# Row transposes ahead of the outputs of the job in front, scatters regrouped, the last job's gates in two halves

## The chip, the cores and the metric

One core of a Trainium2 chip runs the kernel. The metric is the device time of one execution in microseconds (us); the time before is the median of three executions. The profile is of one further execution, and its own time stands beside it below.

## What is computed

Eight sequences of 512 tokens, 256 wide, go through four residual layers: attention to a 64-token context, a router that sends 384 of 512 tokens of each sequence through a gelu block, a second attention, and a mixture of eight experts of which each token uses two. The change touches the last layer alone:

```
x = hidden_states.reshape(-1, H)
probs = softmax(x @ gate_w.T)
w, idx = top_k(probs, 2)
w = w / sum(w)
combine = zeros((T, E)).at[arange(T)[:, None], idx].add(w)
def step(acc, inputs):
    gup, dn, ce = inputs
    g, u = split(x @ gup.T, 2)
    return acc + ce[:, None] * (silu(g) * u @ dn.T), None
```

All numbers are float32. The tokens are the 4096 rows of x, an expert's hidden width is 1024.

## The kernel before

**Rows and jobs.** When a batch (a sequence) has passed the second attention, its last steps, the route steps, write its rows into a table `xs` in HBM that is sorted by expert, and the plain rows into the output. Each row carries its token number, its expert and two weights beside the 256 values. `sent_off(t, k)` (L816) is one such scatter of 128 rows, issued by POOL as an indirect DMA; there are eight for each batch. The expert layer is then made of jobs: a job reads 256 rows of one expert (fewer in the small jobs), multiplies them with that expert's weights and adds the weighted result into the output by an indirect DMA from POOL (`add_rows`, L106).

**Early and late jobs.** Seven early jobs work on rows of the first four batches while the last four batches are still in the layers before. 18 late full jobs, seven jobs of 128 rows and ten pairs of 64 rows follow when every batch is through.

**The steps of an early job** (`early_steps`) are: `load` (SP reads two registers from the job list and issues the DMA of the rows into `e_xg`), four `load_piece` and one `load_down` (weights), then `enter` (TensorE transposes the rows into PSUM at L1111, ACT copies them to `e_xT` at L1114, VectorE makes token numbers and weights), four `gates` (two slices `gate_up` each, L1135, with L1143 on ACT and L1144 and L1145 on VectorE behind it), then `down(0)` and `down(1)` (the outputs: eight matmuls each at L1162, a scaling on VectorE at L1170, `add_rows` on POOL). There is one `e_xg`, one `e_xT`, one `e_hT` and one set of weights.

**The order.** All that happens up to the late jobs stands in an order written out by hand, the string `ORDER`. Each letter takes the next step of a chain: a digit is the attention, route and scatter chain of a batch, `j` the chain of the early jobs, `l` the making of the two job lists. `in_order` ties the instructions of each step behind those of the step before on TensorE, VectorE, ACT and POOL. A scatter also waits for the last TensorE instruction that stands before it in this order (`products[-1:]`). The SP queue issues its DMAs in the order of the program.

**The first late job.** `load(0, late=True)` issues the two halves of `wgu` (the gate and up weights, L1300), then the rows `xg` (L1277), then `wdn` (L1306); the rows wait until the eight scatters of the last batch have landed (`routed`). Then `enter(order[0], ...)` transposes them (L1317, ACT copy L1319) behind the last output of the last early job, and the gates of the late jobs (L1349, L1357, L1358) begin. Outputs of late jobs are `down` (L1406, L1414, L106).

**The late loop** takes each job in turn: its gates, the `enter` of the job after it, then the outputs of the job before it. So the last job's gates all stand before the outputs of the job in front of it, and its own outputs end the kernel. The first three jobs are pinned with `in_order`.

**Behind the last batch** POOL also writes zero rows into `xs` (L1032, L1034: the tails), which the rows of the pairs wait for (`tail_sent`).

Of the kernel before, what the change touches and what calls it, by code (L numbers as in the profile page):

```python
# [8 lines left out]
F32 = mybir.dt.float32  # L9
I32 = mybir.dt.int32  # L10
AF = mybir.ActivationFunctionType
ALU = mybir.AluOpType
# [3 lines left out]
P = 128  # L16
# [3 lines left out]
D = 256  # L20
H = 16
DK = 16
NC = D // P
# [4 lines left out]
E = 8  # L28
TOPK = 2
FF = 1024  # L30
NF = FF // P
# [4 lines left out]
RW = D + 4  # L36
# [18 lines left out]
64345645256352452222F36F35F63F222246455635547335546357453674356647435356733333556646v7l6  # L55
3333476G464jj77j5jGj666j5j7jj47Gjjj765j7457j4G5j64654j7j6556747j5j7644644444j76sH6jj5644
44j557j76j7j57jj7Hsj76jjjjHH7565j65jj676jj7jj6j57j5j6j75557j5555jj7j6j667j55557jjjs67j66
j76j7676j66j76s66667j7jjjj7jj6666j77j7j7jjjjj77jjs7j7j7j7j7j777jj77jjjljj77jj77jj
"""


# [1 line left out]
def xattn_ffn_kernel(ctx: ExitStack, tc: tile.TileContext, a: dict, out: bass.AP):  # L63
# [53 lines left out]
    with ExitStack() as front:  # L117
# [931 lines left out]
        def part_of_room(*shape):  # L1049
            n = 1  # L1050
            for k in shape:
                n *= k
            v = room[:, took[0] : took[0] + n]
            took[0] += n
            names = " ".join("abc"[: len(shape)])
            return v.rearrange(f"p ({names}) -> p {names}", **dict(zip("abc", shape)))
# [2 lines left out]
        e_xg = part_of_room(2, RW)  # L1059
        e_xT = part_of_room(NC, 2, P)  # L1060
        e_sg = [part_of_room(1, 2 * P)]
        e_now = keep.tile([P, 2, D], F32, name="e_now")
        e_w = {}
        piece = 2 * P

# [127 lines left out]
        chains["l"] = [early_list, full_list]  # L1193
        chains["j"] = early = []
        jobs_steps = [early_steps(j) for j in range(NEARLY)]
        early += jobs_steps[0][0]
        for j, (_, steps) in enumerate(jobs_steps):

            loads = list(jobs_steps[j + 1][0]) if j + 1 < NEARLY else []
            for n, step in enumerate(steps):  # L1200
                early.append(step)
                if loads and n != len(steps) - 2:
                    early.append(loads.pop(0))


        engines = (
# [5 lines left out]
        def in_order(step):  # L1212
            traced = nc.cur_bb.bb.instructions
            last = traced[-1].name
            step()
            made = []
            for i in reversed(nc.cur_bb.bb.instructions):
                if i.name == last:
                    break
                made.append(i)  # L1220
            for i in reversed(made):
                if i.engine not in engines:
                    continue
# [29 lines left out]
    def kind(j):  # L1253
        return "full" if j < NLATE else "one" if j < NLATE + NONE else "pair"

    def load(j, late=False):

        what = kind(j)
        subs, n = (2 if what == "full" else 1), (2 if what == "pair" else 1)
        first = j if what != "pair" else NLATE + NONE + 2 * (j - NLATE - NONE)  # L1260
        size = P if what != "pair" else P // 2

        with tc.issue_after(last.pop().ins) if last else nullcontext():
            at = [
                (
                    nc.sync.value_load(
                        jobs[0:1, 0, u : u + 1], min_val=0, max_val=E * QROWS + P - subs * size
                    ),
                    nc.sync.value_load(jobs[0:1, 1, u : u + 1], min_val=0, max_val=E - 1),
                )  # L1270
                for u in range(first, first + n)
            ]
        xg = moe.tile([P, 2, RW], F32, tag="xg", name=f"xg_{j}", bufs=3)

        def rows():
            for u, (row, _) in enumerate(at):
                i = nc.sync.dma_start(  # L1277
                    xg[u * size : u * size + size, 0:subs, :],
                    xs[bass.ds(row, subs * size), :].rearrange("(s p) w -> p s w", p=size),
                ).ins  # L1280

                if what == "pair":
                    after(i, tail_sent)
                else:
                    for other in tail_sent:
                        tc.declare_no_dep(i, other, reason="rows of tokens alone")
                    after(i, routed)

        if not late:
            rows()  # L1290
        w = []
        for u in range(n):
            pool = wpool[sets[0] % 4]
            sets[0] += 1
            wgu = pool.tile([P, NC, 2 * FF], F32, tag="wgu", name=f"wgu_{j}_{u}")
            wdn = pool.tile([P, NF, D], F32, tag="wdn", name=f"wdn_{j}_{u}")
            w.append((wgu, wdn))
        for (_, e), (wgu, _) in zip(at, w):
            for c in range(NC):
                nc.sync.dma_start(  # L1300
                    wgu[:, c, :], gu_t[bass.ds(e, 1), :, c, :].rearrange("e p o -> (e p) o")
                )
        if late:
            rows()
        for (_, e), (_, wdn) in zip(at, w):
            i = nc.sync.dma_start(wdn, dn_t[bass.ds(e, 1), :, :, :].rearrange("e p f o -> (e p) f o"))  # L1306
        last.append(i)
        return xg, w
# [31 lines left out]
    def gate_up_full(j, xT, w, hT=None, chunks=range(NF)):  # L1340
        wgu = w[0][0]
        if hT is None:
            hT = moe.tile([P, NF, 2 * P], F32, tag="hT", name=f"hT_{j}")
        for f in chunks:
            ps = ps_gu.tile([P, 2, 2 * P], F32, tag="gu", name=f"gu_{j}_{f}")
            for half in range(2):
                o = half * FF + f * P
                for c in range(NC):
                    nc.tensor.matmul(  # L1349
                        ps[:, half, :],  # L1350
                        lhsT=wgu[:, c, o : o + P],
                        rhs=xT[:, c].rearrange("p s q -> p (s q)"),
                        start=(c == 0),
                        stop=(c == NC - 1),
                    )
# [80 lines left out]
    assert sorted(order) == [j for j in range(NJOB) if j != spare]  # L1436

    def load_at(i):
        return load(order[i], i == 0) if i < len(order) else None

    loads = [load_at(0), load_at(1)]
    entered = []
    in_order(lambda: entered.append(enter(order[0], loads[0][0])))

    def placed(i, step):

        if i < NPIN:
            got = []
            in_order(lambda: got.append(step()))
            return got[0]  # L1450
        return step()

    pending = None
    for i, j in enumerate(order):
        w = loads.pop(0)[1]
        xT, tok, wt = entered.pop(0)
        if i > 0:
            loads.append(load_at(i + 2))
        if i == 0:

            hT = placed(i, lambda: gate_up_full(j, xT, w, None, range(NF // 2)))
            entered.append(placed(i, lambda: enter(order[1], loads[0][0])))
            placed(i, lambda: gate_up_full(j, xT, w, hT, range(NF // 2, NF)))
        elif j < NLATE:
            hT = placed(i, lambda: gate_up_full(j, xT, w))
        else:
            h, hT = placed(i, lambda: gate_up_rows(j, xT, w))
        if i == 0:
            small_list()
            unit_list()  # L1470
            loads.append(load_at(2))
        if 0 < i < len(order) - 1:
            entered.append(placed(i, lambda: enter(order[i + 1], loads[0][0])))
        if pending is not None:
            placed(i, lambda: down(*pending))
        if j >= NLATE:
            placed(i, lambda: turn(j, h, hT))
        pending = (j, hT, w, tok, wt)
# [55 lines left out]
```

## Time and profile before

| | us |
|---|---|
| median of three runs | 1164.99 (1164.78 to 1166.47) |
| the profiled execution's own time | 1173.17 |
| its span, first to last instruction | 1171.5 |
| TensorE (PE) busy | 1146.6 |
| VectorE (DVE) busy | 574.6 |
| ScalarE (ACT) busy | 372.9 |
| GpSimd (POOL) busy | 283.5 |
| gates of late full jobs, L1349, 1152 matmuls | 252.0 |
| outputs of late jobs, L1406, 1008 matmuls | 189.2 |
| gates of early jobs, L1135, 448 matmuls | 101.8 |
| adding rows into the output, L106, `now` | 98.5 (POOL) |
| scatters of rows into `xs`, L816 | 63.3 (POOL) |

All times of the profile count from the start of the span. A line of a timeline gives the start, the time taken, the engine, the line of the code, the operation, the tile written and those read, the shape, the number of instructions merged into the line (a float32 product appears as two matmuls), and in brackets the engine's idle time before it and what ended it. An engine name with a q is its instruction queue: SPq lines are issues of DMAs, not transfers. PEld is the loading of weights into TensorE. A window line gives, for a stretch of time, each engine's busy time and instructions in the order PE, PEld, DVE, ACT, POOL, then the clock that TensorE was granted (1.00 is full), and the share and rate of the DMA engines.

### The profile page before, as it was taken

How to read it: one execution, taken by the hardware profiler on the slowest of the kernel's cores; microseconds unless marked ns; L12 is line 12 of the kernel's file. 1: busy time of each engine (PE TensorE's matmuls, PEld its weight loads, DVE VectorE, ACT ScalarE, POOL GpSimd, SP SyncE). 2: the span in 40 equal slices, each digit the busy share in tenths (PEclk: the TensorE clock that was granted, in tenths of full speed). 3: DMA queues.
4: the chain of work that ended last, by engine and by line, in shares of the span. 5: the costliest groups of instructions: out<-in, count | busy, mean ns of one | idle time of the engine just before them, and what ended most of it. 6: DMA issues, size and time to landing. Idle time of an engine off the chain costs nothing. (4 is left out here: it accounts for less than half of the span.)

```text
span 1171.5 us, 20900 instructions
## 1 busy us (share of the span) xinstructions
PE 1146.6 (98%) x8010; PEld 825.0 (70%) x8010; DVE 574.6 (49%) x1664; ACT 372.9 (32%) x713; POOL 283.5 (24%) x307
## 2 busy tenths in 40 slices
PE   7999999999999999999999999999999999999997
PEld 3565666656657777778787876777767777677786
DVE  6898888878878676556722221221212222222211
ACT  3655645645543433232121121221111211112210
POOL 5331134123440411431412112112121121211212
PEclk9999999999999999999999999999999999999999
DMA  9000001010125344445789688896889967987711
GB/s 270 2 1 2 1 20 38 19 56 20 38 86 165 105 138 115 136 145 163 207 329 353 237 295 293 303 312 224 288 290 330 312 214 272 314 309 237 279 14 19
DMA packets 119988, 203.53 MB, mean 174 GB/s; under 512 B 10608, under 2 KB 105712, under 8 KB 108368
## 3 DMA queue, kind: packets, MB, share of 16 engines
q1 hardware_dynamic: 100048, 179.35, 43.5%
q0 software_dynamic: 14496, 17.86, 7.5%
q10 hardware_dynamic: 5344, 4.98, 1.3%
q8 instruction: 64, 1.05, 0.4%
q14 instruction: 36, 0.29, 0.1%
HBM read 180.38 MB, written 23.47 MB: 174 GB/s over the span
## 5 line engine op out<-in xcount | busy, mean ns | idle before, releaser
L1349 PE MATMUL gu<-xjT,wgu 128*128 128x256 f32 x1152 | 252.0, 379 | 0.7 <-ACT xjT L1319 0.7
L1349 PEld LDWEIGHTS gu<-xjT,wgu 128*128 128x128 f32 x1152 | 217.6, 190 | 31.0 <-issue 1.2
L106 POOL DMA_INDIRECT out_dram<-now,tok x63 | 98.5, 1564 | 474.6 <-DVE now L1414 296.4
L1406 PE MATMUL o<-wdn,hT 128*128 128x256 f32 (+1 forms) x1008 | 189.2, 380 | 0.0
L1406 PEld LDWEIGHTS o<-wdn,hT 128*128 128x128 f32 (+1 forms) x1008 | 151.1, 173 | 28.3 <-issue 1.7
L1358 DVE TENSOR_TENSOR hT<-sg,gu 128x256 f32<-128x256 f32 x144 | 60.6, 421 | 190.6 <-ACT sg L1357 186.7
L1357 ACT ACTIVATE sg<-gu 128x256 f32<-128x256 f32 x144 | 55.3, 384 | 208.5 <-PE gu L1349 205.7
L1376 PE MATMUL gr<-wgu,xjT 128*64 128x512 f32 (+1 forms) x432 | 120.8, 596 | 0.0
L1135 PE MATMUL gu_e<-x_sb,e_wgu 128*128 128x256 f32 x448 | 101.8, 382 | 0.8 <-ACT x_sb L1114 0.6
L1135 PEld LDWEIGHTS gu_e<-x_sb,e_wgu 128*128 128x128 f32 x448 | 83.8, 190 | 15.9 <-issue 2.8
L1414 DVE TENSOR_SCALAR now<-o,wt 128x256 f32<-128x256 f32 x53 | 25.6, 483 | 137.1 <-PE o L1406 137.1
L1376 PEld LDWEIGHTS gr<-wgu,xjT 128*64 128x64 f32 (+1 forms) x432 | 42.8, 150 | 68.4 <-issue 67.0
L390 POOL TENSOR_TENSOR rstd<-ve,mhalf 128x4 f32<-128x4 f32 x32 | 33.0, 1031 | 233.0 <-DVE ve L388 185.4
L816 POOL DMA_INDIRECT xs<-xr,slots x64 | 63.3, 989 | 105.0 <-issue 35.3
L483 DVE TENSOR_REDUCE mx<-sc 128x32 f32<-128x2048 f32 x32 | 73.2, 2287 | 21.4 <-PE sc L476 17.9
L1386 DVE TENSOR_TENSOR h<-sg,gr 128x512 f32<-128x512 f32 x34 | 23.4, 687 | 83.5 <-PE gr L1376 83.4
L446 PE MATMUL ps_q<-xT,w_wq 128*128 128x512 f32 x128 | 62.0, 612 | 0.5 <-ACT xT L417 0.5
L577 PE MATMUL py<-w_wo,cT 128*128 128x256 f32 x256 | 60.3, 384 | 0.0
L1385 ACT ACTIVATE sg<-gr 128x512 f32<-128x512 f32 x34 | 20.3, 597 | 124.7 <-PE gr L1376 124.7
L577 PEld LDWEIGHTS py<-w_wo,cT 128*128 128x128 f32 x256 | 47.3, 190 | 11.7 <-issue 5.3
L399 ACT ACTIVATE xn<-x_sb,shift,rstd 128x256 f32<-128x256 f32 x96 | 49.8, 594 | 17.9 <-DVE shift L396 16.6
L385 DVE BATCH_NORM_STATS2 st<-x_sb 128x6 f32<-128x256 f32 x128 | 51.3, 401 | 4.9 <-DMA x_sb<-in_x_dram 4.8
(286 smaller groups left out, 1455.8 us busy)
## 6 DMA issues: line engine op xcount, KB each, us to landing
wgu<-in_guT_dram SPq DMA_DIRECT2D x90, 1024.0 KB
wdn<-in_dnT_dram SPq DMA_DIRECT2D x45, 1024.0 KB
e_wgu<-in_guT_dram SPq DMA_DIRECT2D x56, 256.0 KB
e_wdn<-in_dnT_dram SPq DMA_DIRECT2D x7, 1024.0 KB
xg<-xs SPq DMA_DIRECT2D x18, 260.0 KB
out_dram<-x_sb ACTq DMA_DIRECT2D x8, 512.0 KB
x_sb<-in_x_dram SPq DMA_DIRECT2D x7, 512.0 KB
x_sb<-xs SPq DMA_DIRECT2D x7, 260.0 KB
```

Source lines behind the costliest of these rows:

```text
L106: i = nc.gpsimd.indirect_dma_start(out=out_rows, out_offset=bass.IndirectOffsetOnAxis(ap=tok, axis=0), in_=rows, in_offset=None, bounds_ch ...
L385: nc.vector.bn_stats(st, x_sb[:, b * TB + t, :])
L446: nc.tensor.matmul(ps, lhsT=w["wq"][:, k, c * P : (c + 1) * P], rhs=got["xT"][:, k, :], start=(k == 0), stop=(k == NC - 1),)
L483: nc.vector.tensor_reduce(got["mx"].rearrange("p t (r h) -> p r t h", r=NQ)[:, :, :, 2 * c : 2 * c + 2], sc, AX.X, ALU.max,)
L577: nc.tensor.matmul(py[:, s, :], lhsT=cT[:, c, t * P : (t + 1) * P], rhs=w["wo"][:, c, :], start=(c == 0), stop=(c == NC - 1),)
L816: i = nc.gpsimd.indirect_dma_start(out=xs, out_offset=bass.IndirectOffsetOnAxis(ap=slots[:, t, k : k + 1], axis=0), in_=xr[:, t, :], in_of ...
L1135: nc.tensor.matmul(ps[:, half, :], lhsT=e_w["gu"][:, c, o : o + P], rhs=e_xT[:, c].rearrange("p s q -> p (s q)"), start=(c == 0), stop=(c ...
L1349: nc.tensor.matmul(ps[:, half, :], lhsT=wgu[:, c, o : o + P], rhs=xT[:, c].rearrange("p s q -> p (s q)"), start=(c == 0), stop=(c == NC - 1),)
L1357: nc.scalar.activation(sg[:, 0 : 2 * P], ps[:, 0, :], AF.Silu)
L1358: nc.vector.tensor_tensor(hT[:, f, :], sg[:, 0 : 2 * P], ps[:, 1, :], ALU.mult)
L1376: nc.tensor.matmul(ps[rows], lhsT=xT[:, c, 0, rows], rhs=wgu[:, c, o : o + 4 * P], start=(c == 0), stop=(c == NC - 1),)
L1406: nc.tensor.matmul(ps[rows], lhsT=hT[:, f, s * P + rows.start : s * P + rows.stop], rhs=wdn[:, f, :], start=(f == 0), stop=(f == NF - 1),)
```

## The change

1. In every early job `enter` is put one step sooner: behind the gates and ahead of the two outputs of the job in front of it. The loads keep their places.
2. The first late job gets its own tiles (`first_xT`, `first_tok`, `first_wt`). Its rows go into `e_xg`: `first_rows` reads the job list and issues them on SP right before the first gates of the last early job, ahead of that late job's `wgu`. `first_enter` transposes them ahead of the last early job's outputs, instead of behind them, with a `ps_m` buffer.
3. The end of `ORDER` is changed. Before, the last eight scatters stood in pairs among the steps of the last two early jobs. Of these eight, now six stand ahead of the outputs of the last but one early job and two behind them; the steps of the last early job have none among them.
4. In the late loop the last job's gates are cut in two halves, with the outputs of the job in front between them.

In the built program this is what moves. On TensorE nothing is added or removed: the four transposes of each `enter` change places with the sixteen matmuls of `down(0)` and `down(1)`, and at the end two outputs stand between gate slices four and five. On SP the rows of the first late job now stand ahead of both `wgu` halves, not behind them. On POOL the order at the end of the early part was scatter 2, output, scatter 2, output, scatter 4, output 2, tails; it is scatter 6, output 2, scatter 2, output, tails, output.

```diff
-j76j7676j66j76s66667j7jjjj7jj6666j77j7j7jjjjj77jjs7j7j7j7j7j777jj77jjjljj77jj77jj
+j76j7676j66j76s66667j7jjjj7jj6666j77j7j7jjjjj77jjs7j7j7j7j7j777j77j77jj77jljjjjjj
...
+        def first_rows():
+            with tc.issue_after(last.pop().ins):
+                first_at.append((
+                    nc.sync.value_load(jobs[0:1, 0, 0:1], ...),
+                    nc.sync.value_load(jobs[0:1, 1, 0:1], ...),
+                ))
+            i = nc.sync.dma_start(
+                e_xg, xs[bass.ds(first_at[0][0], 2 * P), :].rearrange("(s p) w -> p s w", p=P)
+            ).ins
+            last.append(i)
...
+            after(i, routed)
+        def first_enter():
+            ps = ps_m.tile([P, NC, 2, P], F32, tag="m", name="ps_e_first")
+            for c in range(NC):
+                for k in range(2):
+                    nc.tensor.transpose(ps[:, c, k, :], e_xg[:, k, c * P : (c + 1) * P], ident)
+            nc.scalar.copy(first_xT, ps)
+            nc.vector.tensor_copy(first_tok, e_xg[:, :, D].bitcast(I32))
...
-        early += jobs_steps[0][0]
+        early += jobs_steps[0][0] + jobs_steps[0][1][:1]
         for j, (_, steps) in enumerate(jobs_steps):
             loads = list(jobs_steps[j + 1][0]) if j + 1 < NEARLY else []
-            for n, step in enumerate(steps):
+            for n, step in enumerate(steps[1:-2]):
+                if loads:
+                    early.append(loads.pop(0))
+                elif n == 0:
+                    step = lambda step=step: (first_rows(), step())
                 early.append(step)
-                if loads and n != len(steps) - 2:
-                    early.append(loads.pop(0))
+            if loads:
+                early.append(loads.pop(0))
+                early.append(jobs_steps[j + 1][1][0])
+                early += steps[-2:] + loads
+            else:
+                early += [lambda step=steps[-2]: (first_enter(), step()), steps[-1]]
...
-        xg = moe.tile([P, 2, RW], F32, tag="xg", name=f"xg_{j}", bufs=3)
+        xg = moe.tile([P, 2, RW], F32, tag="xg", name=f"xg_{j}", bufs=3) if j > 0 else None
...
-    in_order(lambda: entered.append(enter(order[0], loads[0][0])))
+    entered = [(first_xT, first_tok, first_wt)]
...
+        elif i == len(order) - 1 and j < NLATE:
+            hT = gate_up_full(j, xT, w, None, range(NF // 2))
+            down(*pending)
+            pending = None
+            gate_up_full(j, xT, w, hT, range(NF // 2, NF))
```

More of the change, by code (lines that the diff above doesn't have):

```diff
@@ L1061, in xattn_ffn_kernel @@
         e_sg = [part_of_room(1, 2 * P)]
+        first_xT = part_of_room(NC, 2, P)
         e_now = keep.tile([P, 2, D], F32, name="e_now")
+        first_tok = keep.tile([P, 2], I32, name="first_tok")
+        first_wt = keep.tile([P, 2], F32, name="first_wt")
+        first_at = []
+        def first_rows():
+            with tc.issue_after(last.pop().ins):
+                first_at.append((
+                    nc.sync.value_load(
+                        jobs[0:1, 0, 0:1], min_val=0, max_val=E * QROWS + P - 2 * P
+                    ),
+                    nc.sync.value_load(jobs[0:1, 1, 0:1], min_val=0, max_val=E - 1),
+                ))
[3 more added lines that the diff above has]
+            last.append(i)
+            for other in tail_sent:
+                apart(i, [other], "rows of tokens alone")
+            after(i, routed)
[6 more added lines that the diff above has]
+            nc.vector.tensor_copy(first_tok, e_xg[:, :, D].bitcast(I32))
+            wt2 = small.tile([P, 2], F32, tag="wt2", name="wt2_first")
+            ej = job_e[:, 0:1]
+            nc.vector.scalar_tensor_tensor(
+                first_wt, e_xg[:, :, D + 1], ej, e_xg[:, :, D + 2], ALU.is_equal, ALU.mult
+            )
+            nc.vector.scalar_tensor_tensor(
+                wt2, e_xg[:, :, D + 1], ej, e_xg[:, :, D + 3], ALU.not_equal, ALU.mult
+            )
+            nc.vector.tensor_tensor(first_wt, first_wt, wt2, ALU.add)
         e_w = {}
@@ L1254, in kind, with load @@
         return "full" if j < NLATE else "one" if j < NLATE + NONE else "pair"
-    def load(j, late=False):
+    def load(j):
         what = kind(j)
@@ L1261, in load @@
         size = P if what != "pair" else P // 2
-        with tc.issue_after(last.pop().ins) if last else nullcontext():
-            at = [
+        with tc.issue_after(last.pop().ins) if last and j > 0 else nullcontext():
+            at = first_at if j == 0 else [
                 (
@@ L1272, in load @@
             ]
-        xg = moe.tile([P, 2, RW], F32, tag="xg", name=f"xg_{j}", bufs=3)
[L1275 to L1290, printed above, removed]
+        xg = moe.tile([P, 2, RW], F32, tag="xg", name=f"xg_{j}", bufs=3) if j > 0 else None
+        for u, (row, _) in enumerate(at) if j > 0 else []:
+            i = nc.sync.dma_start(
+                xg[u * size : u * size + size, 0:subs, :],
+                xs[bass.ds(row, subs * size), :].rearrange("(s p) w -> p s w", p=size),
+            ).ins
+            if what == "pair":
+                after(i, tail_sent)
+            else:
+                for other in tail_sent:
+                    tc.declare_no_dep(i, other, reason="rows of tokens alone")
+                after(i, routed)
         w = []
@@ L1302, in load @@
                 )
-        if late:
-            rows()
         for (_, e), (_, wdn) in zip(at, w):
@@ L1438, in load_at @@
     def load_at(i):
-        return load(order[i], i == 0) if i < len(order) else None
+        return load(order[i]) if i < len(order) else None
     loads = [load_at(0), load_at(1)]
-    entered = []
-    in_order(lambda: entered.append(enter(order[0], loads[0][0])))
+    entered = [(first_xT, first_tok, first_wt)]
     def placed(i, step):
```

## The prediction

> **What bounds the kernel now.** I read the busy table first, then the timeline of TensorE where the early part ends, then POOL's and SP's at the same place, then the last ten microseconds.
>
> ```profile
> PE 1146.6 (98%) x8010; PEld 825.0 (70%) x8010; DVE 574.6 (49%) x1664; ACT 372.9 (32%) x713; POOL 283.5 (24%) x307
> ```
>
> TensorE is the bound: 1146.6 of 1171.5 us. The change adds and removes no matmul, so it can only gain or lose in the 24.9 us that are left. 5.2 of these lie before the first matmul and 7.3 behind the last. The rest are holes. From 400 us on, the timeline of TensorE shows three of more than a third of a microsecond, and they sit where the change works:
>
> ```profile
> 551.17 7.07 PE L1162 MATMUL o_e<-e_wdn,x_sb 128*128 128x256 f32 x32
> 558.07 0.60 PE L1111 MATMUL ps_e<-ident,x_sb 128*128 128x128 f32 x4
> ...
> 559.40 14.21 PE L1135 MATMUL gu_e<-x_sb,e_wgu 128*128 128x256 f32 x64 [0.61 <-ACT x_sb L1114]
> 573.46 7.43 PE L1162 MATMUL o_e<-e_wdn,x_sb 128*128 128x256 f32 x32
> 581.67 0.63 PE L1317 MATMUL ps_x<-ident,xg 128*128 128x128 f32 x4 [0.79 <-DMA xg<-xs]
> 582.97 7.17 PE L1349 MATMUL gu<-xjT,wgu 128*128 128x256 f32 x32 [0.68 <-ACT xjT L1319]
> ```
>
> The gates of the last early job wait 0.61 us for the copy of its transposes. The first late job waits 0.79 for its rows and 0.68 for its copy. Behind 582.97 TensorE is never idle until the end (50.00 of each 50 us), so whatever moves that start moves the end by the same amount.
>
> **What the whole change could gain.** Had the first late job nothing to wait for, its gates would start at 558.80 (where the last early job's gates can begin: outputs, transposes and one small counting product are the same work in either order and end there today, 0.61 ahead of 559.40) + 14.06 (those gates, 559.40 to 573.46) + 0.44 (four transposes, start to start as 558.07 to 558.51) + 6.90 (two outputs, 551.17 to 558.07) = 580.20 against 582.97: 2.8 us. That is all there is.
>
> **Part 1, the early jobs' transposes one step sooner.** In jobs two to six other products stand between the transposes and the gates, and the only such hole in the trace is the 0.61 us. It goes: gates start at 558.80 and TensorE reaches 572.85, not 573.46. Rows of those jobs are loaded a whole job ahead (job seven's: issued at 535.90, used at 558.07, now at 551.2), so no wait replaces it. VectorE's five small instructions (558.68 to 559.67, 1.0 us) move ahead of the two scalings; these wait 1.0 us longer, hidden by POOL, which takes them later anyway (below). If that cover were gone it would cost POOL 1.0 us.
>
> **Parts 2 and 3, rows of the first late job and the scatters.** This is the expensive part.
>
> ```profile
> 557.33 1.05 POOL L816 DMA_INDIRECT xs<-xr,slots  x1 [20.92 <-issue]
> 558.68 1.01 POOL L816 DMA_INDIRECT xs<-xr,slots  x1 [0.30 <-PE ps_e L1111]
> 560.00 1.62 POOL L106 DMA_INDIRECT out_dram<-e_now,tok_e  x1 [0.31 <-DVE cnt_f L915]
> ...
> 575.66 0.96 POOL L816 DMA_INDIRECT xs<-xr,slots  x1 [0.30 <-issue]
> ```
>
> ```profile
> 567.01 0.91 SPq L1300 DMA_DIRECT2D wgu<-in_guT_dram  x2
> 578.62 0.39 SPq L1277 DMA_DIRECT2D xg<-xs  x1
> ```
>
> The rows may be read once the eighth scatter has landed. It starts at 575.66, ends at 576.62, and SP issues the rows at 578.62: 2.00 us. Their transposes start at 581.67: another 3.05. Today the scatters are held back by products of the last early job; afterwards they follow one another. The first cannot be sooner: VectorE finishes the slots and columns at 556.45, unchanged. So: scatter one 557.33, two 1.35 later, three to six every 1.28 (561.93 to 563.22 is 1.29, 410.60 behind 409.33 is 1.27): six starts at 563.80 and ends at 564.76. Then two outputs of 1.62 with 0.30 before each: 568.60. Scatter seven 568.90, eight 570.17, ending 571.13; it starts 5.5 sooner than now. SP issues the rows at 573.13, and the transposes can start at 576.18.
>
> But TensorE now comes to these transposes at 572.85, ahead of 6.90 us of outputs that would have covered the wait. It stands 3.33 us, with the outputs queued behind the transposes. Then 576.18 + 0.44 + 6.90 = 583.52: the copy is hidden, and the gates still begin 0.55 later than now. The 0.37 us by which the outputs of the last early job take longer today (7.43 against 7.07) go too; 580.20 above has that in it. Bounds: the first scatter starts 0.88 behind VectorE, an output at 1133.92 only 0.28 behind (1133.64), so at best 0.6 sooner; a landing that holds up POOL at the end takes from 1159.66 to 1163.27, 3.61 instead of 2.00, so at worst 1.6 later. I take the sum's own row, the same scatter with no weights in flight.
>
> **The clock.** A long hole on TensorE has a price of its own:
>
> ```profile
> 16.92 1.17 PE L476 MATMUL sc<-kbd,qT 32*128 32x128 f32 x32
> ...
> 21.30 0.33 PE L414 MATMUL ps_x<-ident,xn 128*128 128x128 f32 x1 [1.29 <-ACT xn L399]
> ...
> 24.03 2.03 PE L476 MATMUL sc<-kbd,qT 32*128 32x128 f32 x32
> ```
>
> ```profile
> 19.04:22.45 3.41, 1.79 (x6) 0.55 (x4) 3.22 (x10) 1.81 (x4) 1.83 (x3) 1.00 1.03 337
> 22.45:25.86 3.41, 3.27 (x38) 2.73 (x37) 2.28 (x3) 1.44 (x3) 3.23 (x7) 0.50 1.08 345
> 237.50:240.91 3.41, 1.95 (x16) 1.05 (x19) 3.38 (x5) 0.00 (x0) 0.61 (x1) 1.00 0.18 65
> ```
>
> In a stretch of 3.41 us TensorE was busy for 1.79; in the next, its granted clock (the column behind the five engines) is 0.50, and 32 small matmuls take 2.03 instead of 1.17. With 1.95 busy it kept its clock. Both stretches lie on one grid of 3.41 us, which also has 571.99, 575.41 and 578.82. A hole from 572.85 to 576.18 leaves 0.86 busy in the first: half clock from 575.41 to 578.82, of which 2.64 us are work, so 1.32 us are lost. Wherever the grid lies, one stretch holds at least 1.67 of the 3.33 us, so the loss is 0.83 to 1.71 (half of 1.67 to 3.41). I take 1.32.
>
> [...]
>
> **The weights** of the first late job stand behind its rows now: issued from 573.7 (0.59 behind the rows, as 578.62 to 579.21 on SP) instead of 567.01. Before, both halves were in by the stretch from 575.41, where the DMA share falls from 0.82 to 0.22: 8.4 to at most 9 us, so 582.1 to 582.7, and the gates need them at 583.5 or, with the clock, 584.8. Nothing, with 0.8 to 2.7 us of cover; each microsecond beyond is one lost. POOL's last output now stands behind the tails; the first to need it landed is the scatter at 616.27.
>
> **Part 4, the end.**
>
> ```profile
> 1160.79 0.48 DVE L1414 TENSOR_SCALAR now<-o,wt 128x256 f32<-128x256 f32 x1 [2.97 <-PE o L1406]
> 1163.27 1.56 POOL L106 DMA_INDIRECT out_dram<-now,tok  x1 [3.61 <-issue]
> 1164.24 0.48 DVE L1414 TENSOR_SCALAR now<-o,wt 128x256 f32<-128x256 f32 x1 [2.97 <-PE o L1406]
> 1165.13 1.56 POOL L106 DMA_INDIRECT out_dram<-now,tok  x1 [0.30 <-DVEq L1483]
> ```
>
> The next to last scatter waits for the job in front to land and so holds POOL until 1164.83; the last starts at 1165.13, 0.41 behind its scaling (1164.72) where 0.28 would do. With the job in front 7 us sooner, 0.13 is gained. The last four slices' tails (0.39 on ACT, 0.42 on VectorE, 0.87 us behind the product at 1150.4) are needed only by the eighth of eight products, 3.0 us in: nothing; 0.9 if uncovered.
>
> **Sum**: +0.55 + 1.32 - 0.13 = +1.74 us on a span of 1171.5, thus 1173.2 (execution 1174.9). The profiled execution is 8.2 us longer than the median; a difference within 25 us of it I carry over as it is: 1164.99 + 1.74 = **1166.7**.
>
> **Rivals.**
> - *The clock falls for two stretches.* The stretch from 575.41 is itself idle for 0.77 us; no row shows whether 77% busy at half clock brings the clock back (96% did, at 25.86). Decides if it doesn't: 3.41/2 = 1.71 more, 1168.4, slower. For it: 57% busy kept the full clock, which speaks against; nothing else.
> - *The weights come late.* Decides past 585.4, 11.7 us behind their issue instead of 8.4 to 9: against it, the two scatters that shared the engines then are gone; for it, the rows' 260 KB go first. 1167.4 and up, slower.
> - *Short hole, no drop.* Outside the profiler POOL may issue faster, as 8.2 us go somewhere. Below about 1.5 us of hole the clock stays: 0.55 - 1.8 - 0.13 = -1.4; with 3.33 and the clock kept +0.42. Between them, 1163.6 to 1165.4, within 0.2% of before.
> - *No hole at all*, the scatters 3.33 us (24% of 13.8) sooner: 1162.1, faster. Against: a chain of fixed spacings.
>
> **How the numbers follow.** One clock stretch 0.42 (1166.2 to 1167.1), two stretches 0.22, weights 0.08, short hole or kept clock 0.18, no hole 0.10. 0.2% (2.3 us) is about what a measurement of this kernel can tell from no change. Within it lie 0.42 + 0.18 = 0.60; slower 0.30; faster 0.10. The range leaves out the fastest case and the worst of the weights: 1164.0 to 1168.8.
>
> **What would show it.** Right: a hole of 3 us at `ps_e_first` released by the DMA of the rows, the last scatter near 570, a stretch of 0.50 clock behind it, gates of the first late job at 584 to 585, no holes behind it. Wrong: that hole under 1.5 us, clock 1.00 throughout, gates before 582, or a hole at the first `gu` released by `wgu`.

## The result: 0.4% slower, and the profile after

| | before | after |
|---|---|---|
| median of the runs of one chip, us | 1165.86 (1164.78 to 1167.04, 6 runs) | 1170.81 (1169.83 to 1171.76, 6 runs) |
| ratio of after to before, 95% interval | | 1.0042 [1.0031, 1.0052] |
| the profiled execution's own time, us | 1173.17 | 1170.64 |
| its span, us | 1171.5 | 1168.9 |
| first gates of the first early job (first `gu_e`), us | 352.61 | 344.34 |
| from there to the first late output (first `o`), us | 258.75 | 264.48 |
| from the first late output to the end of the last matmul, us | 552.85 | 552.84 |

The change costs 4.95 us (3.6 to 6.1). The two profiled executions say the opposite at first sight, since the span after is the shorter. But before its first early gates, where both kernels run the same instructions, the execution of before was 8.3 us behind. The stretch that the change touches, from the first early gates to the first late output, took 258.75 us before and 264.48 after. I call it *the way* below, and compare kernels by it; what lies behind it is equal to 0.01 us up to the last matmul.

The first line of the page's busy table, of the kernel after:

```profile
PE 1145.0 (98%) x8010; PEld 823.8 (70%) x8010; DVE 574.5 (49%) x1664; ACT 372.7 (32%) x713; POOL 282.9 (24%) x307
```

Same matmuls, same engine as the bound. What is new are holes. The timeline of TensorE after has them at the outputs and transposes of jobs in the middle of the early part, which the prediction had down as free of waits:

```profile
375.62 1.14 PE L414 MATMUL ps_x<-ident,xn 128*128 128x128 f32 x8 [0.50 <-ACT x_sb L1152]
...
453.88 2.43 PE L1200 MATMUL o_e<-e_wdn,x_sb 128*128 128x256 f32 x10 [0.86 <-DVE e_now L1208]
...
483.34 1.07 PE L476 MATMUL sc<-kbd,qT 32*128 32x128 f32 x32
484.34 0.64 PE L715 MATMUL ps_g<-xT,gwT 128*32 128x128 f32 x16
484.91 0.65 PE L1149 MATMUL ps_e<-ident,x_sb 128*128 128x128 f32 x4
486.82 0.66 PE L491 MATMUL pm<-ident,mx 128*128 128x128 f32 x4 [1.25 <-DVE mx L483]
```

The same place of the third hole in the timeline of before, and the reduction that `pm` waits for, in VectorE's timeline after:

```profile
490.47 1.07 PE L476 MATMUL sc<-kbd,qT 32*128 32x128 f32 x32
491.46 0.64 PE L715 MATMUL ps_g<-xT,gwT 128*32 128x128 f32 x16
492.04 3.72 PE L1162 MATMUL o_e<-e_wdn,x_sb 128*128 128x256 f32 x16
495.60 0.60 PE L491 MATMUL pm<-ident,mx 128*128 128x128 f32 x4
```

```profile
484.47 2.29 DVE L483 TENSOR_REDUCE mx<-sc 128x32 f32<-128x2048 f32 x1 [0.29 <-PE sc L476]
```

Between the scores `sc` and the transposes `pm` of their maxima, VectorE needs 2.29 us. Before, the first output of an early job, 3.6 us long, stood there and covered them. After, the four transposes `ps_e` stand there, 0.5 us long. That is what putting `enter` one step sooner does in this kernel: the letters of `ORDER` keep their places, so `enter` takes the letter of `down(0)`, `down(0)` that of `down(1)`, and `down(1)` that of the load behind it, other batches' steps between. The last load (`load_down`) takes the letter that `enter` had, so not every load keeps its place. The outputs come later, and the reduction that they used to cover is bare.

The other two holes have the same origin, but what is waited for there is a buffer in PSUM, where this kernel has its products written. ACT's and VectorE's lines that end them, in the kernel after:

```profile
375.00 0.56 ACT L1152 COPY x_sb<-ps_e 128x512 f32<-128x512 f32 x1
```

```profile
453.35 0.48 DVE L1208 TENSOR_SCALAR e_now<-o_e,wt_e 128x256 f32<-128x256 f32 x1
```

The products named in these two cases take their buffers in turn from one pool of four, `ps_m`, so by the program each takes the buffer of the fourth product before it. Both start right behind the instruction that reads that product, 0.06 and 0.05 us behind its end. `ps_x` at 375.62 reads nothing of the early rows, but three buffers (`ctx`, `pz`, `ctx`) were taken between `ps_e` and it, and the copy of `ps_e` ends at 375.56. The second output at 453.88 has three buffers (`ps_x`, `pc`, `ps_x`) between the first output and itself, and the scaling of the first ends at 453.83. Before, the two outputs of that job had only `bz` between them. This is read from the program and the trace; no run changed the number of buffers.

The end of the early part after: TensorE, then POOL's last scatter, SP's issue of the rows, and the last scaling on VectorE.

```profile
561.14 7.17 PE L1173 MATMUL gu_e<-x_sb,e_wgu 128*128 128x256 f32 x32 [0.29 <-DVE x_sb L1183]
570.50 1.09 PE L1089 MATMUL ps_e_first<-ident,x_sb 128*128 128x128 f32 x4 [2.19 <-DMA x_sb<-xs]
571.38 8.30 PE L1200 MATMUL o_e<-e_wdn,x_sb 128*128 128x256 f32 x32
580.46 7.14 PE L1389 MATMUL gu<-x_sb,wgu 128*128 128x256 f32 x32 [0.78 <-DVE e_now L1208]
```

```profile
564.79 1.00 POOL L816 DMA_INDIRECT xs<-xr,slots  x1 [0.30 <-issue]
```

```profile
567.68 0.38 SPq L1077 DMA_DIRECT2D x_sb<-xs  x1
568.33 0.91 SPq L1342 DMA_DIRECT2D wgu<-in_guT_dram  x2
```

```profile
579.72 0.48 DVE L1208 TENSOR_SCALAR e_now<-o_e,wt_e 128x256 f32<-128x256 f32 x1 [0.88 <-PE o_e L1200]
```

The foreseen hole is there, 2.19 us instead of 3.33. The rows were issued 1.89 us behind the last scatter's end (565.79) and used 2.82 later. Behind the hole the outputs take 8.30 us, not 7.07. Then comes a hole that the prediction did not have: the first late gates wait 0.78 us for the scaling of the last output, which makes neither their rows nor their weights. The windows of that place:

```profile
567.04:570.45 3.41, 1.27 (x6) 0.77 (x5) 3.29 (x14) 0.87 (x3) 0.00 (x0) 1.00 0.50 131
570.45:573.86 3.41, 3.36 (x10) 2.93 (x11) 2.21 (x12) 0.59 (x1) 0.00 (x0) 0.50 0.99 413
573.86:577.27 3.41, 3.41 (x17) 2.98 (x16) 1.00 (x5) 0.00 (x0) 0.24 (x1) 1.00 1.00 365
```

One stretch with the clock at 0.50 (the column behind the five engines), as foreseen, and only one.

### The profile page after: what moved, and what is told of

Same layout as the page of the kernel before. It is cut to its first block, busy times and chain, and to the rows that moved or that the text cites. A ratio compares the mean times of both kernels' runs of the same rounds, so it can differ in the third digit from the quotient of the medians.

```text
span 1168.9 us, 20905 instructions
## 1 busy us (share of the span) xinstructions
PE 1145.0 (98%) x8010; PEld 823.8 (70%) x8010; DVE 574.5 (49%) x1664; ACT 372.7 (32%) x713; POOL 282.9 (24%) x307
## 5 line engine op out<-in xcount | busy, mean ns | idle before, releaser
L1389 PE MATMUL gu<-xjT,wgu 128*128 128x256 f32 x1088 | 238.1, 379 | 0.0
L1389 PEld LDWEIGHTS gu<-xjT,wgu 128*128 128x128 f32 x1088 | 205.6, 190 | 28.5 <-issue 1.2
L106 POOL DMA_INDIRECT out_dram<-now,tok x61 | 95.0, 1558 | 450.7 <-DVE now L1454 306.6
```

The source lines that it names most:

```text
L106: i = nc.gpsimd.indirect_dma_start(out=out_rows, out_offset=bass.IndirectOffsetOnAxis(ap=tok, axis=0), in_=rows, in_offset=None, bounds_ch ...
L1389: nc.tensor.matmul(ps[:, half, :], lhsT=wgu[:, c, o : o + P], rhs=xT[:, c].rearrange("p s q -> p (s q)"), start=(c == 0), stop=(c == NC - 1),)
```

## The experiments

Theory 1, as it was put down before the first of these runs: part 1 costs 1.5 to 2.5 us, since outputs stand one letter later and no longer cover what they covered; parts 2 and 3 cost 2.5 to 3.3 us, for the rows, the clock and a PSUM buffer; part 4 costs nothing. The runs were made in three groups, each on a chip of its own and with the kernel before beside it (medians of 1172.0, 1174.0 and 1172.3 us); each ratio is to the before of its own group. The table collects them; "way" and "idle" (TensorE's idle time within the way) are of each kernel's own profiled execution.

| kernel | way, us | idle, us | ratio to before, 95% |
|---|---|---|---|
| before, the trace shown | 258.75 | 3.57 | |
| before again | 257.93 | 3.04 | 0.9998 [0.9987, 1.0009] |
| part 4 alone | 258.32 | 3.15 | 1.0006 [0.9994, 1.0017] |
| part 1 alone | 262.06 | 5.67 | 1.0042 [1.0030, 1.0053] |
| part 1 alone, again | 261.81 | 5.59 | 1.0038 [1.0023, 1.0053] |
| parts 2 and 3 alone | 259.67 | 4.94 | 1.0028 [1.0017, 1.0038] |
| parts 2 and 3 alone, again | 259.69 | 4.78 | 1.0009 [1.0000, 1.0018] |
| the whole change, the trace shown | 264.48 | 7.14 | 1.0042 [1.0031, 1.0052] |
| the whole change, again | 263.49 | 7.48 | 1.0041 [1.0026, 1.0056] |
| the whole, TensorE kept busy in the hole | 263.73 | 5.38 | 1.0034 [1.0021, 1.0047] |
| the whole, other PSUM layout | 262.10 | 6.33 | 1.0035 [1.0025, 1.0046] |
| part 1 with outputs at their letters | 258.53 | 3.09 | 0.9993 [0.9984, 1.0003] |
| parts 2 and 3, transposes between the outputs | 258.58 | 2.94 | 0.9990 [0.9979, 1.0001] |
| the last with two more edits | 258.34 | 2.93 | 1.0001 [0.9991, 1.0011] |

The first three ways, whose kernels are alike up to the first late output, have a mean of 258.33 and lie within 0.8 us: that is how far a way can be trusted.

### Before again, and each part alone

The first is the kernel before, unchanged. The second has only the reordering of the chain `j`, the third `first_rows`, `first_enter`, the new `load` and the scatters grouped as in the change (at the end of `ORDER` the letters `j` stand a little differently than in the change, the order on POOL is the same), with `enter` of the early jobs where it was, the fourth only the two halves of the last job's gates.

```diff
 part 1 alone
-        early += jobs_steps[0][0]
+        early += jobs_steps[0][0] + jobs_steps[0][1][:1]
...
+                early.append(jobs_steps[j + 1][1][0])
+            early += steps[-2:] + loads
 parts 2 and 3 alone
+            if not loads:
+                steps[1] = lambda step=steps[1]: (first_rows(), step())
+                steps[-2] = lambda step=steps[-2]: (first_enter(), step())
```

> The kernel before, unchanged: a second profile of it. Its profiled execution took 1173.17 us against a median of 1165; lined up with the profile after on the same matmuls, it had lost 8.2 us by 348 us, where nothing is changed yet. If that was one execution's bad luck (a half-clock stretch at 22.45, holes at 238 and 347), this profile's span is 1162 to 1165 and its first gates of a late job start near 575. If the profiler itself costs the kernel before 8 us, the span is near 1171 again. Timed, it shows what the comparison makes of no change: within 0.1%.

> Part 1 alone: the early jobs' transposes one step sooner, and with them both outputs and the last load one letter later; the end of the order, the first late job and the last job as before. Theory (new holes in the early part): the profile after shows holes of 0.50 (transposes of another batch wait for the copy of the early rows), 0.86 (an output waits for the scaling of the one before), 1.25 (a transposing of maxima waits for VectorE's maximum) and 0.25, together 2.9, and saves 0.6: +1.5 to +2.5 us, with these holes. Rival (the prediction's sum): nothing but 0.61 saved, -0.6 to 0 us, and the whole 4.95 us come from the first late job.

> Parts 2 and 3 alone: early transposes behind the outputs as before, last scatters and rows of the first late job as in the change, the last job as before. Theory: a hole of about 2 us at the first late job's transposes, half clock for one stretch, and a wait of about 0.8 behind the last output: +2.5 to +3.3 us. Rival (all of it lies here): +5. Rival (the prediction's sum): +1.9.

> Part 4 alone: the last job's gates in two halves. Both theories: 0 to -0.3 us, the end of the span 6.3 to 6.5 us behind the last matmul plus 0.9.

The kernel before again has a span of 1169.9 us, and its profiled execution (1171.66) is no slower than the others of its group, so the profiler itself does not cost 8 us here. Why the executions of the first timing stayed near 1165 is open.

Part 1 alone, by its timing, is as slow as the whole change, 1.0042 [1.0030, 1.0053]: 4.9 us of 1172, about twice what was expected of it (+1.5 to +2.5). Its trace has the holes of the whole change at `ps_x` (0.50), the second output and `pm`, and no longer the 0.61:

```profile
460.27 3.72 PE L1162 MATMUL o_e<-e_wdn,x_sb 128*128 128x256 f32 x16 [0.88 <-DVE e_now L1170]
...
493.53 0.66 PE L491 MATMUL pm<-ident,mx 128*128 128x128 f32 x4 [1.25 <-DVE mx L483]
```

Parts 2 and 3 alone have the other two, but not the half clock that was expected there:

```profile
577.38 0.63 PE L1089 MATMUL ps_e_first<-ident,x_sb 128*128 128x128 f32 x4 [2.50 <-DMA x_sb<-xs]
577.85 7.07 PE L1200 MATMUL o_e<-e_wdn,x_sb 128*128 128x256 f32 x32
585.70 7.15 PE L1383 MATMUL gu<-x_sb,wgu 128*128 128x256 f32 x32 [0.78 <-DVE e_now L1208]
```

Part 4 alone can't be told from before. So the prediction's free part is the dearest. Since 4.9 and 3.3 came to more than the whole, part 1 and parts 2 and 3 were run again:

> Part 1 alone once more, since the two parts alone (+4.9 and +3.3 us) came to more than the whole (+4.9). In the trace the way from the first gates of the early jobs to the first late output was 3.7 us longer than in the three traces of before on record (262.06 against 257.93 to 258.75). If the trace is right, +3 to +4.5 us (1.0026 to 1.0038) and a way of 261.5 to 262.6; if the timed runs were, +4.5 to +6.

> Parts 2 and 3 alone once more. In the trace the same way was only 1.3 us longer than before (259.67 against 257.93 to 258.75), the timed runs said 3.3. If the parts add, as the traces say (3.7 + 1.3 = 5.1 against 5.2 to 6.2 for the whole), this is +1 to +2.5 us (1.0009 to 1.0021), the upper end where the clock falls behind the hole; if the timed runs were right, +2.5 to +4 again, and something outside that stretch is slower.

> The whole change on the chip of the other runs. If the costs of part 1 alone (+4.9 us) and of parts 2 and 3 alone (+3.3) simply add, it is +7 to +9 us against before. If they overlap, because the 0.79 and 0.68 us waits of the first late job can only be lost once and because a later start of one wait hides another, it is +4.5 to +6, as on the first chip (+4.95). Same holes either way: 1.1 at ps_x, 0.9 at the second o_e, 1.2 at pm, about 2.2 at ps_e_first, 0.8 at the first gu of the late jobs.

The ways repeat: part 1 adds 3.5 and 3.7 us to the mean of 258.33, parts 2 and 3 add 1.3 and 1.4, together 5.0, and the whole adds 5.2 here and 6.2 in the first trace, the only one with the clock drop behind that hole. In the traces the parts add, then. The second timing of parts 2 and 3 (1.0009) fits that, and the first (1.0028) does not; why it was higher stays open. Part 1's timings (+4.9 and +4.5 us, with lower ends of 3.5 and 2.7) allow the 3.6 of the traces. Of these 3.6 us, 2.4 are idle time (5.6 against 3.25, the mean of the three). The other 1.2 are busy time of TensorE (256.3 us against 255.1), whose cause is not shown: `ctx` and `pz` are among what takes longer (7.05 us against 6.37, and 7.00 against 6.41), but they do so too in the next experiment (6.91 and 6.97), whose way is not longer.

### Part 1 with the outputs left at their letters

`enter` of each early job is merged into the step of `down(0)` of the job in front, right ahead of it. The letter that it had before does nothing, so outputs and loads stand where they stood.

```diff
+            if loads:
+                nxt = jobs_steps[j + 1][1]
+                steps[-2] = lambda one=nxt[0], two=steps[-2]: (one(), two())
+                nxt[0] = lambda: None
```

> Before, with the transposes of each early job directly ahead of the first output of the job in front of it, and outputs and loads at the letters where they stood before. Theory 1 (the loss of part 1 comes from outputs that stand one letter later): the 1.2 us hole at pm and the 0.9 us hole between the two outputs are gone, the 0.61 us hole as well; -0.8 to +0.8 us against before, 0.9993 to 1.0007. Rival (the loss comes from transposes ahead of outputs in themselves: their PSUM buffer and their five VectorE instructions in front of the scaling): the holes stay, +2.5 to +5 us, 1.002 to 1.004.

The timeline of TensorE at the third hole, of this kernel:

```profile
488.97 1.07 PE L476 MATMUL sc<-kbd,qT 32*128 32x128 f32 x32
489.97 0.65 PE L715 MATMUL ps_g<-xT,gwT 128*32 128x128 f32 x16
490.55 0.66 PE L1111 MATMUL ps_e<-ident,x_sb 128*128 128x128 f32 x4
491.04 3.62 PE L1162 MATMUL o_e<-e_wdn,x_sb 128*128 128x256 f32 x16
494.49 0.60 PE L491 MATMUL pm<-ident,mx 128*128 128x128 f32 x4
```

Transposes ahead of the output, and the output again between `sc` and `pm`: the holes of 0.50, 0.86 and 1.25 are gone, and so is the 0.61. Waits of 0.33 and 0.25 come up. The way is 258.53, 3.4 us shorter than with part 1 as it was written, with the same instructions and the same transposes ahead of the outputs. The rival, that transposes ahead of outputs cost in themselves, is out; it is the shift of the outputs. (The last load is back at its letter too, but none of part 1's holes ends with a DMA of weights.) Against before (0.9993 [0.9984, 1.0003]) nothing can be told.

### The clock behind the hole

Twenty transposes of the identity stand ahead of the real ones, so that TensorE has work while the rows come. Their result is overwritten.

```diff
+            for _ in range(20):
+                nc.tensor.transpose(ps[:, 0, 0, :], ident, ident)
```

> The whole change, with 20 further transposes of the identity on TensorE, whose results are overwritten, ahead of the first late job's transposes, so that TensorE is busy while it waits for the rows. If the half clock behind that hole costs what the profile shows (outputs 8.30 us instead of 7.07), this kernel is 0.8 to 1.7 us faster than the whole change on this chip and its outputs there take 7.1 us. If the clock falls in a few executions only, or costs nothing, the two are within 0.5 us of each other.

TensorE's timeline of this kernel:

```profile
575.91 2.35 PE L1088 MATMUL ps_e_first<-ident 128*128 128x128 f32 x20
578.10 0.60 PE L1091 MATMUL ps_e_first<-ident,x_sb 128*128 128x128 f32 x4
578.53 7.07 PE L1202 MATMUL o_e<-e_wdn,x_sb 128*128 128x256 f32 x32
586.39 3.91 PE L1391 MATMUL gu<-x_sb,wgu 128*128 128x256 f32 x17 [0.78 <-DVE e_now L1210]
```

No hole at the transposes, full clock, outputs of 7.07. But the way, 263.73, is not shorter than the whole change's 263.49 on this chip, and the timed ratios overlap. One reason is that the clock had not fallen in the whole change's trace on this chip either. Another is that twenty are too many: SP issued the rows at 574.69, and the real transposes start 3.41 us behind that, where the five traces without them have 2.75 to 2.90. So this run prices the extra transposes at some 0.6 us (an estimate from these rows) and says little about the price of a half clock. The windows around the hole of the whole change, run again:

```profile
576.67:580.08 3.41, 2.45 (x12) 1.77 (x10) 3.22 (x19) 0.77 (x3) 0.00 (x0) 1.00 0.24 56
580.08:583.50 3.42, 2.18 (x12) 2.02 (x13) 3.35 (x16) 1.24 (x3) 0.00 (x0) 1.00 1.06 382
```

This hole of 2.20 us lies over two stretches (2.45 and 2.18 busy) as they are laid here, and the clock stayed at 1.00; behind the one of 2.19 that lay in one stretch (1.27 busy) it was 0.50. Where the stretches begin in this trace is the author's estimate, as no half clock in its rows fixes an edge. Of five traces with that hole (the whole change twice, with the other PSUM layout, parts 2 and 3 twice) one has the drop. How often it falls without a profile, these runs can't say.

### The PSUM buffer of the first late gates

In the whole change `ps_gu` and `ps_x` change places, so that the first late gates write to a part of PSUM that no early output holds.

```diff
     ps_o = ctx.enter_context(tc.tile_pool(name="ps_o", bufs=2, space=PSUM))
-    ps_gu = ctx.enter_context(tc.tile_pool(name="ps_gu", bufs=4, space=PSUM))
     ps_x = ctx.enter_context(tc.tile_pool(name="ps_x", bufs=2, space=PSUM))
+    ps_gu = ctx.enter_context(tc.tile_pool(name="ps_gu", bufs=4, space=PSUM))
```

> The whole change with the PSUM buffers of the late gates and those of the transposes exchanged, so that the first late gates write to banks that no output holds. Theory (that hole is the wait for a buffer which the last scaling releases): the hole of 0.8 us ahead of the first gates of the late jobs is gone, nothing else changes, 0.8 us faster than the whole change, 1.0034 against before where that had 1.0041. Rival (it is the scaling's result or the weights that they wait for): the hole stays.

```profile
580.79 0.63 PE L1089 MATMUL ps_e_first<-ident,x_sb 128*128 128x128 f32 x4 [2.25 <-DVE ex_u L882]
581.26 7.07 PE L1200 MATMUL o_e<-e_wdn,x_sb 128*128 128x256 f32 x32
588.17 7.07 PE L1389 MATMUL gu<-x_sb,wgu 128*128 128x256 f32 x32
```

In TensorE's timeline the gates follow the outputs at once (588.17, no bracket), where the same change with the old layout waited 0.87. It was the buffer: neither the weights nor the scaled result had changed. The way is 1.4 us shorter, 0.5 more than that hole accounts for and within what a way can be trusted; the timing doesn't tell the two apart. (The releaser in the first line, a VectorE list instruction, is inferred by the profile; in three of the five traces with this hole it names the DMA of the rows. In all five the transposes start 2.75 to 2.90 us behind SP's issue of the rows, so it is the rows that they wait for.)

### Transposes between the outputs

Parts 2 and 3 alone, with the other PSUM layout and `first_enter` ahead of `down(1)`, not of `down(0)`. The lines below are the second of these; the first is the exchange shown above.

```diff
-                steps[-2] = lambda step=steps[-2]: (first_enter(), step())
+                steps[-1] = lambda step=steps[-1]: (first_enter(), step())
```

> Parts 2 and 3 alone, but with the first late job's transposes between the two outputs of the last early job, not ahead of both, and with the PSUM buffers of the late gates laid on banks that came free long before. Theory (the cost of parts 2 and 3 is the wait for the rows plus the wait for a PSUM buffer that the last scaling has to release): the outputs cover the rows, a hole of at most 0.5 us is left at ps_e_first, none at the first gu; -0.5 to -2 us against before, 0.9983 to 0.9996. Rival (the regrouped scatters cost elsewhere, in VectorE or POOL): +1 to +3 us, 1.001 to 1.003, with no large hole there.

Its timeline of TensorE:

```profile
572.84 3.49 PE L1200 MATMUL o_e<-e_wdn,x_sb 128*128 128x256 f32 x14
577.13 0.70 PE L1200 MATMUL o_e<-e_wdn,x_sb 128*128 128x256 f32 x2 [0.81 <-DVE x_sb L1183]
577.67 0.60 PE L1089 MATMUL ps_e_first<-ident,x_sb 128*128 128x128 f32 x4
578.10 3.62 PE L1200 MATMUL o_e<-e_wdn,x_sb 128*128 128x256 f32 x16
581.56 1.67 PE L1383 MATMUL gu<-x_sb,wgu 128*128 128x256 f32 x6
```

One output is cover enough: no wait for rows, none for a copy, none for a buffer. The 2.50 and 0.78 us are gone, and 1.1 us of the way with them (258.58 against 259.67). What is left is a wait inside the first output for the last gates' VectorE work, 0.81 here; the 7.43 us of that line before, 0.36 above the 7.07 of others, may hold some of the same. To take that away too, the last job list was put behind the last early gates on VectorE, and the last early job's `enter` merged as above:

```diff
+            if j == NEARLY - 2:
+                nxt = jobs_steps[j + 1][1]
+                steps[-2] = lambda one=nxt[0], two=steps[-2]: (one(), two())
+                nxt[0] = lambda: None
...
+            tc.add_manual_dep(first_unit, last_half[0].name, ...)
```

> The kernel with the first late job's transposes between the two outputs and the other PSUM layout, with two more edits: the transposes of the last early job stand directly ahead of the first output of the job in front (its 0.61 us wait for the copy goes, 0.25 may come in its place), and VectorE's making of the last job list stands behind the last early gates (the 0.81 us that the first output waited for VectorE goes). Theory: 0.8 to 1.4 us faster than without the two edits (0.999), so 0.9975 to 0.9985 against before, no hole above 0.3 us from 550 us on. Rival (a hole that goes is replaced by the next wait, for the rows): a hole of 0.5 to 1 us at ps_e_first and 0.999 again.

```profile
578.53 0.70 PE L1201 MATMUL o_e<-e_wdn,x_sb 128*128 128x256 f32 x2 [0.66 <-DVE x_sb L1184]
579.07 0.60 PE L1089 MATMUL ps_e_first<-ident,x_sb 128*128 128x128 f32 x4
...
583.88 6.74 PE L1388 MATMUL gu<-x_sb,wgu 128*128 128x256 f32 x30 [0.32 <-DMA wgu<-in_guT_dram]
```

A miss. The wait went from 0.81 to 0.66 only, so the last list was not its cause; what it is stays open. And as TensorE comes sooner to the late gates (their first at 582.96, 8.15 us behind SP's issue of their weights at 574.81, where the kernel without the two edits had 8.58), it waits 0.32 there for weights. The rival had the kind right, a hole that goes is replaced by the next, but named the wrong one. No kernel tried is faster than before by more than its interval.

## Why the prediction was wrong, step by step

- **Part 1, "no wait replaces it".** This is the step that failed: costed at -0.61 us, measured at +3.5 and +3.7 on the way. The working looked at what `enter` waits for (its rows, the 0.61 for its copy) and at the scalings behind it on VectorE. It took the exchange as one between neighbours on TensorE, which holds for the last early job alone, and even there two waits of 0.25 and 0.26 came in place of the 0.61. In the other jobs steps of other batches stand between the letters. There the outputs moved away from a reduction that they covered (1.25 us at `pm`), and two products met a PSUM buffer that had not been read yet (0.86 at the second output, 0.50 at `ps_x`). The prediction asked what is late for the step that is moved, not what the steps that make room had been covering. Merging the transposes into the output's letter took the cost back, which shows it.
- **Parts 2 and 3, the hole.** The mechanism was right, its size was not: 3.33 us forecast, 2.19, 2.20, 2.25 and 2.50 measured, and 1.51 in parts 2 and 3 again, where the gates ahead of it had waited another 0.62 for VectorE. In the first trace the landing of scatter (1.89 for 2.00) and rows (2.82 for 3.05) gives 0.34 of the 1.14 us missing. The rest is the distance from the eighth scatter's start to TensorE's arrival at the transposes, 3.52 us (564.79 to 568.31) where the sum had 2.68 (570.17 to 572.85).
- **"The copy is hidden."** It was; but with transposes and copy gone from between the last output and the first gates, the gates meet a PSUM buffer that the last scaling had not released, 0.78 us. Before, the 0.68 us wait for the copy stood in that place. The prediction did not look for it.
- **The clock.** One stretch of half clock behind the hole, where and as long as forecast: outputs of 8.30 us for 7.07 and transposes of 0.88, start to start, for 0.44 make 1.67 against 1.32. In the other four traces with that hole it did not come. So the term was right for one execution and too dear as a mean.
- **Weights, part 4.** No late gates of the whole change wait for weights in either trace. Part 4 was put at -0.13; its ratio, 1.0006 [0.9994, 1.0017], can't tell that from nothing.
- **The sum.** From the last early gates' start to the first late gates the forecast was 24.72 us (558.80 to 583.52) and 1.32 for the clock, 26.04; measured 26.76 (553.70 to 580.46), 23.57 before. A hole forecast 1.14 too long stands against 0.78 for the buffer, 0.35 of clock, and gates that took 14.61 to TensorE's arrival instead of 14.05, so that by luck most of these errors cancel and 0.72 is left: with part 1's 0.61 as forecast the total would have been 1164.99 - 0.61 + 3.19 (26.76 less 23.57) = 1167.6, inside the range. Part 1 took it out. The rivals were all of parts 2 and 3: none asked whether the outputs' move costs something, so the chance of slower was too low.

## What to carry to other kernels

In an order written by hand, a step that moves ahead pushes others back: for each of these, look in the trace for what runs on the other engines beside it and would be bare without it, not only for what the moved step waits for. Long products (here outputs of 3.6 us) are cover, and short ones in their slot (0.5 us) are not; keep the long ones where the wait is and merge the short ones next to them. Where buffers are taken in turn, count too which product's buffer each one gets in the new order, and when that is read. Where two profiled executions differ ahead of the change by more than the change is worth, line them up at the first instruction that is touched.

## What was not expected of the chip

In these traces the busy share of a stretch did not decide the clock by itself. Behind the stretch that the prediction went by, with 1.79 us busy of 3.41, the clock was 0.50. Parts 2 and 3 alone kept 1.00 behind one with 1.78, and the kernel before, run again, had 0.50 behind one with 2.71, in which the matmuls were small ones of 32 rows:

```profile
573.10:576.51 3.41, 1.78 (x9) 1.22 (x7) 2.96 (x16) 1.08 (x3) 0.00 (x0) 1.00 0.39 96
576.51:579.92 3.41, 2.54 (x14) 2.34 (x15) 3.40 (x16) 0.97 (x2) 0.00 (x0) 1.00 1.04 390
```

```profile
246.62:250.03 3.41, 2.71 (x37) 1.84 (x32) 0.98 (x4) 0.23 (x1) 2.09 (x2) 1.00 0.32 117
250.03:253.44 3.41, 3.41 (x41) 1.78 (x41) 2.29 (x1) 2.54 (x5) 0.00 (x0) 0.50 0.02 5
```

The first fence is the windows of parts 2 and 3 alone, the second those of the kernel before, run again; the clock is the column behind the five engines. In the trace of parts 2 and 3 again the stretches lie on one grid: its windows from 21.90 to 25.31, 25.31 to 28.73 and 254.01 to 257.42 have a clock of 0.50, and from 21.90 to 254.01 it is 232.11 us, 68 stretches of 3.4133. The window with 1.78 lies 161 of these behind 23.56, where a half clock begins in its own trace (23.56 to 26.98). The stretch with 2.71 has 0.70 idle in all, so the prediction's rival of a short hole, with the clock kept below about 1.5 us of hole, has a row against it. Of the two holes of 2.2 us, the one within a stretch (1.27 busy) had 0.50 behind it, the one across two, by the estimate above, 1.00. What is counted as busy, these runs leave open.

The part that no edit touches moved more than the edits: the first early gates began between 344.34 and 355.88 us in the 14 traces. Some of it is half-clock stretches near 23 and 250 us, which come in some executions only: the trace with 344.34, that shown of after, has the clock at 1.00 up to 570.4, the one with 355.88, parts 2 and 3 again, has the three stretches of 0.50 named above. The timed intervals here are some 2.5 us wide, which that may explain in part, and the way in the trace told the parts apart where the timings could not.
